# First group of a state-space decoder layer: two pairs of chunks from tokens without the row scale

## Chip, cores and metric

The kernel runs on one core of a Trainium2 chip. The metric is device time in microseconds, the median of three runs. Engines: PE (TensorE matmul, its weight loads shown as PEld), DVE (VectorE), ACT (ScalarE), POOL (GpSimd) and SP, whose queue issues all DMAs that matter here.

## What is computed

A decoder layer on 16 sequences of 256 tokens with 512 features, all float32, in three parts: a state-space block, a long convolution against a context, and a feed-forward layer with low-rank experts. The change lies in the start of the first part:

```python
xn = x * rsqrt(mean(x * x, axis=-1) + EPS) * w_norm       # row scale per token, wn per feature
proj = einsum('bld,td->blt', xn, W_in)
z, xi, dt, Bm, Cm = split(proj)                            # 1024, 1024, 16, 256, 256 columns
xi = silu(causal_conv4(xi))                                # per column, 4 taps along the tokens
dt = softplus(dt + dt_bias); dA = exp(-dt * exp(A_log))
u = (dt * mean of xi per head) * Bm
h = dA * h + u ; y = sum(h * Cm)                           # scan along the tokens
out = (y @ W_h2i.T * silu(z)) @ W_out.T + x                # then x + out, layer norm
```

The row scale is one number per token. It commutes with the product over features, so it can multiply the projected columns too.

## The kernel before

**Groups.** The first part runs over eight groups of 512 tokens (two sequences). In a group the projection is done with the tokens along the free axis: `xnT` holds the turned x, 128 features x 4 x 512 tokens. Columns are handled in pairs of 128-column chunks, in an order written out by hand; for the first group it is x0, x1, z0, x2, z1, x3, b0, c1, z2, z3 (L660 to L663). "x1" is the second pair of `xi` columns, with chunks 2 and 3, and so on.

**A pair.** Each pair is a 2 x 2 block product with seven products in place of eight: two chunks, two sequences, two halves of the features. `A11`, `S1`, `S2`, `S3`, `A12`, `S4`, `A22` are the weights and their sums, the S made by POOL in `weight_sums` (L259); "11", "12", "21", "22" are the quarters of xnT and T1 to T4 differences of them (L250 to L257). A product is four matmul instructions of 128 x 256 in the trace. `first_products` (L375) does A11, S1, S2, S3 into two PSUM banks `al`, `be`; `first_sums` (L385) reads them, one ACT copy and three DVE sums (L388, L389, L390); `last_products` (L393) adds A12, S4, A22 onto the same banks; `last_sums` (L399) reads them (ACT L400, DVE L401, L402).

**Order.** The scheduler is off: each engine executes in the order of the code. In iteration i of the loop at L686 PE gets the first products of pair i and then the last products of pair i-1; DVE gets the first sums of pair i, then the last sums of pair i-1 (`finish_sums`, L671). For an x pair `mixed` (L614) follows for both its chunks: the four-tap convolution, the first tap by DVE (L621, even chunk) or ACT (L619, odd chunk), three more by DVE (L623). `al` and `be` come from two pools: two banks for every third pair, four for the others.

**Weight sums of POOL.** Those of x0, x1, z0 and x2 are made in front, the others in iterations 1, 2 and 4, each behind a wait for the last L623 of a pair (L748).

**The front of the first group.** SP issues four DMAs of x rows (`xt`, L227, for the mean squares), `wn` (L269), the low and high half of the turned x with the first two weights between (L272 to L275), then w_z 0 and the rest. PE runs idle matmuls (L521). `rms` (L404) squares the rows on ACT and DVE and takes the power -1/2 on POOL (L419); `along_tokens` (L422) turns the scale into a PSUM tile `rt` that holds it along the free axis; `normed` (L444) multiplies xnT by wn and rt (L446). `decays` (L452) makes dt and dA, its matmuls `d` (L460) on PE in iteration 1, its further steps in iterations 2, 3 and 4.

Of the kernel before, what the change touches and what calls it, by code (L numbers as in the profile page):

```python
# [8 lines left out]
F32 = mybir.dt.float32  # L9
# [5 lines left out]
P = 128  # L15
# [10 lines left out]
GT = 512  # L26
# [27 lines left out]
)  # L54
ER = NE * R
NG = NE + ER
WARM = 8


def layer_norm_stats(nc, pool, nhalf, src, tag):  # L60
# [13 lines left out]
def decoder_kernel(  # L74
# [135 lines left out]
    with ExitStack() as s1:  # L210
# [12 lines left out]
        def load_x(g):  # L223
            xs = []
            for t in range(TT):
                xt = xp.tile([P, D], F32, tag="xt", name="xt")
                nc.sync.dma_start(xt, xg[g * TT + t])  # L227
                xs.append(xt)
            return xs
# [17 lines left out]

        A11, A12, A22, S3, S1, S2, S4 = range(7)

        def first_token_sum(eng):  # L250
            eng.tensor_tensor(Xs["T1"], Xs["12"], Xs["11"], ALU.subtract)  # L251

        def other_token_sums(eng):
            eng.tensor_tensor(Xs["T2"], Xs["22"], Xs["T1"], ALU.subtract)  # L254
            eng.tensor_tensor(Xs["T3"], Xs["22"], Xs["12"], ALU.subtract)

            eng.tensor_tensor(Xs["T4"], Xs["21"], Xs["T2"], ALU.subtract)  # L257

        def weight_sums(eng, w, p):  # L259

            ins = eng.tensor_tensor(w[:, p, S1], w[:, p, S3], w[:, p, A22], ALU.add)
            eng.tensor_tensor(w[:, p, S2], w[:, p, S1], w[:, p, A11], ALU.subtract)
            eng.tensor_tensor(w[:, p, S3], w[:, p, A11], w[:, p, S3], ALU.subtract)
            eng.tensor_tensor(w[:, p, S4], w[:, p, A12], w[:, p, S2], ALU.subtract)
            return ins

        xs_next = load_x(0)
        wn = wp.tile([P, KD], F32, name="wn")
        nc.sync.dma_start(wn, w_norm)  # L269
        w_xi = big.tile([P, NI // 2, 7, 2, P], F32, tag="big", name="w_xi")  # L270
        w_z = big.tile([P, NI // 2, 7, 2, P], F32, tag="big", name="w_z")
        nc.sync.dma_start(xnT[:, 0:2], xTg[:, 0:2, 0:GT])  # L272
        nc.sync.dma_start(w_xi[:, 0, 0:4], Wxi[:, 0])
        nc.sync.dma_start(xnT[:, 2:4], xTg[:, 2:4, 0:GT])
        nc.sync.dma_start(w_xi[:, 1, 0:4], Wxi[:, 1])  # L275
        nc.sync.dma_start(w_z[:, 0, 0:4], Wz[:, 0])
        for p in range(2, NI // 2):
            nc.sync.dma_start(w_xi[:, p, 0:4], Wxi[:, p])
# [74 lines left out]
        def bank():  # L353
            return ps_mm.tile([P, 512], F32, tag="mm", name="mm")

        def product(ps, w, p, a, b, start=False, stop=False, upon=False):
            for kc in range(2):
                nc.tensor.matmul(  # L358
                    ps,
                    w[:, p, a, kc, :],  # L360
                    Xs[b][:, kc, :],
                    start=start and kc == 0,
                    stop=stop and kc == 1,
                    skip_group_check=upon,
                )

        def begin_products(w, p, third):

            al, be = [
                ps_s.tile([P, 512], F32, tag="s", name="s") if third else bank() for _ in range(2)  # L370
            ]
            product(al[:, 0:S], w, p, A11, "11", start=True)
            return al, be

        def first_products(w, p, third, begun=None, between=None):  # L375

            al, be = begun or begin_products(w, p, third)
            product(be[:, 0:S], w, p, S1, "T1", start=True)
            if between is not None:
                between()  # L380
            product(al[:, S:], w, p, S2, "T2", stop=True)
            product(be[:, S:], w, p, S3, "T3", stop=True)
            return al, be
# [20 lines left out]
        def rms(xs, both=False):  # L404

            n = len(xs)
            ss = p2.tile([P, TT], F32, tag="ss", name="ss")[:, 0:n]
            for t in range(n):
                sq = p2.tile([P, D], F32, tag="acc", name="sq", bufs=6)
                if both and t % 2:  # L410
                    nc.vector.scalar_tensor_tensor(
                        sq, xs[t], 1.0, xs[t], ALU.mult, ALU.mult, accum_out=ss[:, t : t + 1]
                    )
                else:
                    nc.scalar.activation(sq, xs[t], AF.Square, accum_out=ss[:, t : t + 1])
            ms = p2.tile([P, TT], F32, tag="ms", name="ms")[:, 0:n]
            nc.vector.tensor_scalar(ms, ss, 1.0 / D, RMS_EPS, ALU.mult, ALU.add)  # L417
            rstd = p2.tile([P, TT], F32, tag="rstd", name="rstd")[:, 0:n]
            nc.gpsimd.tensor_tensor(rstd, ms, nhalf[:, 0:n], ALU.pow)  # L419
            return rstd  # L420

        def along_tokens(ps, rstd):  # L422

            for t in range(2):
                nc.tensor.matmul(
                    ps[:, t * P : (t + 1) * P],
                    rstd[:, t : t + 1].to_broadcast([P, P]),
                    ident,
                    start=True,
                    stop=True,  # L430
                )
# [12 lines left out]
        def normed(rt, kcs=range(KD)):  # L444
            for kc in kcs:
                nc.vector.scalar_tensor_tensor(  # L446
                    xnT[:, kc, :], xnT[:, kc, :], wn[:, kc : kc + 1], rt, ALU.mult, ALU.mult
                )
# [68 lines left out]
        def idle(n):  # L517

            ps = bank()
            for _ in range(n):  # L520
                nc.tensor.matmul(ps[:, 0:P], ident, ident, start=True, stop=True)  # L521


        rt = ps_t.tile([P, GT], F32, tag="tr", name="rt")
        idle(WARM)
        for b in range(GB):
            along_tokens(
                rt[:, b * S : (b + 1) * S], rms(xs_next[b * TT // GB : (b + 1) * TT // GB], True)
            )
            idle(WARM // 2)  # L530
        normed(rt, (0, 1))
        first_token_sum(nc.vector)
        normed(rt, (2, 3))
        other_token_sums(nc.vector)
        for w, p in ((w_xi, 0), (w_xi, 1), (w_z, 0), (w_xi, 2)):
            weight_sums(nc.gpsimd, w, p)

        later = {
            1: ((w_z, 1),), 2: ((w_xi, 3), (w_bc, 0), (w_bc, 1)), 4: ((w_z, 2), (w_z, 3)),
# [48 lines left out]
        for g in range(groups):  # L588
# [25 lines left out]
            def mixed(c):  # L614

                xi = xis[c % 4]
                acc = p2.tile([P, GB, S], F32, tag="acc", name="acc", bufs=6)
                if c % 2:
                    nc.scalar.activation(acc, xi[:, :, 3:], AF.Identity, scale=wc[:, c, 3:4])  # L619
                else:  # L620
                    nc.vector.tensor_scalar(acc, xi[:, :, 3:], wc[:, c, 3:4], None, ALU.mult)  # L621
                for k in range(2, -1, -1):
                    ins = nc.vector.scalar_tensor_tensor(  # L623
                        acc, xi[:, :, k : k + S], wc[:, c, k : k + 1], acc, ALU.mult, ALU.add
                    )
                mixes.append(ins)
                accs.append(acc)
                silus.append(acc)
# [33 lines left out]
                order[1:3] = order[2:0:-1]  # L662
            order += [("b", 0), ("c", 1), ("z", 2), ("z", 3)]  # L663
            before = None
            begun = []

            def finish_products():
                kind, p, al, be, u, to = before
                last_products(al, be, kinds[kind], p)
# [16 lines left out]
            for i, (kind, p) in enumerate(order):  # L686
# [4 lines left out]
                    sums.append((w, cols, chunk_sum(w, cols)))  # L691
                if i == 6:
                    ms = [head_means(0)]
                if g == 0 and i == 0:
                    al, be = first_products(
                        kinds[kind], p, True, None,
                        lambda: begun.append(begin_products(w_xi, order[1][1], False)),
                    )
                else:
                    al, be = first_products(  # L700
                        kinds[kind], p, i % 3 == 0, begun.pop(0) if begun else None
                    )
                if i == 8:
                    ms.append(head_means(1))
                if i == 9:
# [11 lines left out]
                            )  # L717
                    if sums:
                        centred(*sums.pop(0))
                if before is not None:  # L720
                    finish_products()
                to = places(kind, p)
                u = first_sums(al, be, to)
                if i == 8:
                    states(1, stepped(ms[1], spreads[2]), spreads[3])
                if i == 6:
                    ms = [stepped(ms[0], spreads[0])]
                    spreads.append(spread(1, 1))
                if g == 0:
                    if i == 1:  # L730
                        parts = decays()
                    if i == 2:
                        nc.scalar.activation(A, A, AF.Exp)
                        nc.vector.tensor_scalar(A, A, -1.0, None, ALU.mult)
                    if i in (1, 2, 4):
                        next(parts)
                if i == 9:
                    yT = q3.tile([P, S], F32, tag="vn", name="yT", bufs=1)
                    nc.scalar.copy(yT, yps)
                if before is not None:  # L740
                    finish_sums((lambda: next(parts)) if g == 0 and i == 2 else None)
                if g == 0 and i == 3:
                    next(parts)
                if g == 0 and i in later:
# [1024 lines left out]
```

## Time and profile before

| | |
|---|---|
| median of three runs | 1398.14 us (1397.74 to 1398.74) |
| profiled execution | 1399.62 us, its span 1397.8 us |
| PE busy | 1379.8 us |
| DVE busy | 1186.5 us |
| POOL busy | 620.2 us |
| ACT busy | 450.2 us |
| granted TensorE clock | 0.998 mean |

Three runs lie within 1 us. The profiled execution is one execution with the profiler on, from which all durations come; its span runs from the first to the last instruction. A busy PE is not PE at its peak, as matmuls overlap and their ends are modelled.

### The profile page before, as it was taken

The numbers are of one execution on the slowest core, as the hardware profiler recorded it, in microseconds if no ns is written. First come the engines' busy times: TensorE is split into PE (matmuls) and PEld (weight loads), VectorE is DVE, ScalarE is ACT, GpSimd is POOL, SyncE is SP. The second block draws the span as 40 slices with busy tenths as digits, with TensorE's granted clock in tenths as the row PEclk, the third lists the DMA queues.
The fourth block names the chain that finished last, engine by engine and source line by source line (L and its number), as shares of the span: only waits on it lengthen the run. The fifth ranks groups of instructions, "written<-read, shape, count | busy, mean of one in ns | idle before, by whom it ended". The sixth has DMA issues, their size and how long they took to land.

```text
span 1397.8 us, 19582 instructions
## 1 busy us (share of the span) xinstructions
PE 1379.8 (99%) x6967; PEld 935.3 (67%) x6967; DVE 1186.5 (85%) x2270; ACT 450.2 (32%) x979; POOL 620.2 (44%) x849
## 2 busy tenths in 40 slices
PE   8999999999999999999999999999999999999997
PEld 7888788788888887888886345445454454545444
DVE  6888879878788787788866889999999999999986
ACT  2524324243243342432421323333323333333232
POOL 5451021020100201001003768877888788887884
PEclk9999999999999999999999999999999999999999
DMA  8113212212113131121306554454543555345500
GB/s 307 34 38 91 63 54 37 69 40 55 39 41 68 49 68 39 41 53 42 80 20 87 69 69 64 60 74 61 76 64 60 74 76 76 61 61 72 65 27 38
DMA packets 362386, 89.48 MB, mean 64 GB/s; under 512 B 330032, under 2 KB 334512, under 8 KB 362288
## 3 DMA queue, kind: packets, MB, share of 16 engines
q1 hardware_dynamic: 362288, 88.23, 34.1%
q8 instruction: 55, 0.90, 0.3%
q14 instruction: 43, 0.35, 0.1%
HBM read 70.62 MB, written 17.58 MB: 63 GB/s over the span
## 4 chain that ended last, share of the span: by engine, by line
PE 94%; DVE 3%; issue 1%; DMA 1%; POOL 0%; ACT 0%; SPq 0%; POOLq 0%; DVEq 0%
PE mm L358 21%; PE y L1088 15%; PE s L358 14%; PE y L1103 12%; PE s L826 6%; PE mm L826 6%; PE y L1070 4%; PE be L1335 4%; PE al L1335 3%; PE gl L1280 2%; PE xm L634 1%; PE mm L783 1%; PE mm L920 1%; PE al L1307 1%; PE s L920 1%
## 5 line engine op out<-in xcount | busy, mean ns | idle before, releaser
L1136 DVE TENSOR_TENSOR pr<-y,cT 128x1024 f32<-128x1024 f32 x126 | 148.4, 1219 | 38.4 <-PE y L1103 37.7
L1103 PE MATMUL y<-kv 64*64 64x512 f32 x1536 | 179.6, 598 | 0.0
L187 DVE TENSOR_TENSOR kv<-tr,cT 128x1024 f32<-128x1024 f32 x128 | 150.0, 1212 | 0.8 <-ACT tr L179 0.8
L623 DVE SCALAR_TENSOR_TENSOR acc<-xi,wc,acc 128x512 f32<-128x512 f32 x192 | 142.8, 757 | 7.4 <-ACT acc L619 1.8
L1146 DVE TENSOR_REDUCE red<-pr 128x128 f32<-128x1024 f32 x126 | 147.1, 1208 | 0.0
L1088 PE MATMUL y<-kv 128*128 128x512 f32 x272 | 128.3, 594 | 3.5 <-DVE pr L1136 3.4
L1103 PEld LDWEIGHTS y<-kv 64*64 64x64 f32 x1536 | 52.2, 132 | 118.6 <-issue 96.7
L69 POOL TENSOR_TENSOR rs_a<-ve_a,nhalf 128x1 f32<-128x1 f32 x32 | 17.5, 546 | 255.3 <-DVE ve_a L67 255.0
L1088 PE MATMUL y<-kv,Td 128*128 128x512 f32 x248 | 116.5, 592 | 0.0
L419 POOL TENSOR_TENSOR rstd<-ms,nhalf 128x4 f32<-128x4 f32 (+1 forms) x9 | 8.6, 954 | 229.7 <-DVE ms L417 229.7
L358 PE MATMUL mm<-XT,w_z 128*128 128x256 f32 x384 | 90.7, 379 | 0.0
L1088 PEld LDWEIGHTS y<-kv,Td 128*128 128x128 f32 x248 | 47.1, 190 | 59.3 <-issue 59.3
L1077 ACT COPY y<-y 64x512 f32<-64x512 f32 x120 | 67.0, 558 | 59.5 <-PE y L1070 57.6
L1088 PEld LDWEIGHTS y<-kv 128*128 128x128 f32 x272 | 51.1, 189 | 44.9 <-ACT y L1077 17.3
L1054 POOL TENSOR_TENSOR xs<-kv 128x512 f32<-128x512 f32 x63 | 80.2, 1273 | 0.1
L358 PEld LDWEIGHTS mm<-XT,w_z 128*128 128x128 f32 x384 | 73.0, 190 | 9.9
L358 PE MATMUL mm<-xnT,w_z 128*128 128x256 f32 x288 | 70.8, 382 | 0.0
L1490 POOL TENSOR_TENSOR ol<-o,red 128x512 f32<-128x512 f32 x31 | 39.3, 1267 | 61.4 <-DVE red L1146 61.4
L251 POOL TENSOR_TENSOR XT<-xnT 128x512 f32<-128x512 f32 x7 | 9.3, 1326 | 129.0 <-PE mm L826 129.0
L1070 PE MATMUL y<-xs,kv 128*128 128x512 f32 x120 | 62.2, 600 | 0.4
L358 PE MATMUL s<-XT,w_xi 128*128 128x256 f32 x256 | 61.0, 380 | 0.8 <-DVE XT L254 0.5
L358 PEld LDWEIGHTS mm<-xnT,w_z 128*128 128x128 f32 x288 | 54.0, 190 | 10.1 <-issue 3.0
(337 smaller groups left out, 3065.6 us busy)
## 6 DMA issues: line engine op xcount, KB each, us to landing
cT<-in_ctxT SPq DMA_DIRECT2D x32, 384.0 KB
kv<-in_toep SPq DMA_DIRECT2D x32, 384.0 KB
xt<-in_x SPq DMA_DIRECT2D x32, 256.0 KB
spread<-both SPq DMA_DIRECT2D x32, 256.0 KB
first<-xt SPq DMA_DIRECT2D x124, 64.0 KB
vT<-first SPq DMA_DIRECT2D x31, 256.0 KB
out<-res SPq DMA_DIRECT2D x31, 256.0 KB
xnT<-in_xT SPq DMA_DIRECT2D x7, 1024.0 KB
```

The lines of the kernel that those rows point to most:

```text
L187: last = nc.vector.tensor_tensor(kv[:, q, k * BQ : (k + NL // 2) * BQ], vT[:, q, blks].rearrange("p k (b i) -> p (k b) i", i=NH).unsqueeze ...
L358: nc.tensor.matmul(ps, w[:, p, a, kc, :], Xs[b][:, kc, :], start=start and kc == 0, stop=stop and kc == 1, skip_group_check=upon,)
L623: ins = nc.vector.scalar_tensor_tensor(acc, xi[:, :, k : k + S], wc[:, c, k : k + 1], acc, ALU.mult, ALU.add)
L826: nc.tensor.matmul(ps, own[a][c][:, n * P : (n + 1) * P], w_o[b][c], start=start and c == 0, stop=stop and c == HC - 1, skip_group_check=upon,
L1054: return nc.gpsimd.tensor_tensor(xs[:, q], moving(kv, q, 0), moving(kv, q, 1), ALU.add)
L1070: nc.tensor.matmul(seed, T[:, SHARED_AT, :], xs[:, q], start=True, stop=True)
L1077: nc.scalar.copy(bank_of(y, 2)[b : b + HP], seed[a : a + HP])
L1088: nc.tensor.matmul(bank_of(y, lb), w, moving(kv, q, mb), start=not late and lb not in begun, stop=False, skip_group_check=True,)
L1103: return nc.tensor.matmul(bank_of(y, lb)[cols], T[rows, DIAGONAL_AT, (b - a) * HP : (b - a + 1) * HP], moving(kv, q, lb)[rows], start=star ...
L1136: nc.vector.tensor_tensor(pr.rearrange("p (k b j) i -> p k b j i", k=2, j=NH), y[i].rearrange("p k (b j i) -> p k b j i", j=NH, i=NH), cT[ ...
L1146: nc.vector.tensor_reduce(red[:, q, 2 * i : 2 * i + 2, :].rearrange("p k t -> p (k t)"), pr, AX.X, ALU.add)
L1335: nc.tensor.matmul(ps, a[:, kc, :], w[:, kc, :], start=(start and kc == 0), stop=(kc == 1), skip_group_check=True,)
```

## The change

Only the first group differs. The turned x is loaded first, into two tiles of its own (`x_lo`, `x_hi`), followed by wn and the first two weights between and behind the halves; the x rows come after these. ACT and DVE multiply the halves by wn, in place. T1 to T4 are made from them, and the pairs x0 and x1 take these tokens, without the row scale. Meanwhile the mean squares are taken on ACT and DVE, after x0's first sums; power and turning follow x0's last products on POOL and PE. POOL makes the weight sums of z0 and x2 behind the power. DVE then multiplies the four rows of tokens by rt into xnT and makes T1 to T4 again; T4 comes between x0's last sums and its `mixed`. The results of x0 and x1 are multiplied by rt in `mixed`, once for each of four chunks, by DVE. In iteration 2, x1's last products stand ahead of z0's first ones, and the `d` matmuls and first two steps of `decays` both fall there. x0's and x1's first products are no longer interleaved; 11 idle matmuls stand in front, and none between.

```diff
-WARM = 8
+WARM = 11
...
+        def given_tokens():
+
+            halves = [gp.tile([P, 2, GT], F32, tag="zs", name="xr") for _ in range(2)]
+            sums = [gp.tile([P, 2, GT], F32, tag="zs", name="xr_sum") for _ in range(2)]
+            X = {
+                f"{k + 1}{b + 1}": t[:, :, b * S : (b + 1) * S]
+                for k, t in enumerate(halves)
+                for b in range(GB)
+            }
+            for i in range(4):
+                X[f"T{i + 1}"] = sums[i // 2][:, i % 2, :].rearrange("p (k s) -> p k s", k=2)
+            return halves, X
...
-        xs_next = load_x(0)
         wn = wp.tile([P, KD], F32, name="wn")
-        nc.sync.dma_start(wn, w_norm)
+        (x_lo, x_hi), Xr = given_tokens()
...
-        nc.sync.dma_start(xnT[:, 0:2], xTg[:, 0:2, 0:GT])
+        nc.sync.dma_start(x_lo, xTg[:, 0:2, 0:GT])
+        nc.sync.dma_start(wn, w_norm)
         nc.sync.dma_start(w_xi[:, 0, 0:4], Wxi[:, 0])
-        nc.sync.dma_start(xnT[:, 2:4], xTg[:, 2:4, 0:GT])
+        nc.sync.dma_start(x_hi, xTg[:, 2:4, 0:GT])
         nc.sync.dma_start(w_xi[:, 1, 0:4], Wxi[:, 1])
+        xs_next = load_x(0)
         nc.sync.dma_start(w_z[:, 0, 0:4], Wz[:, 0])
...
+        unscaled = {0, 1}
+
         def product(ps, w, p, a, b, start=False, stop=False, upon=False):
+            X = Xr if w is w_xi and p in unscaled else Xs
...
-        rt = ps_t.tile([P, GT], F32, tag="tr", name="rt")
         idle(WARM)
-        for b in range(GB):
-            along_tokens(
-                rt[:, b * S : (b + 1) * S], rms(xs_next[b * TT // GB : (b + 1) * TT // GB], True)
-            )
-            idle(WARM // 2)
-        normed(rt, (0, 1))
-        first_token_sum(nc.vector)
-        normed(rt, (2, 3))
-        other_token_sums(nc.vector)
-        for w, p in ((w_xi, 0), (w_xi, 1), (w_z, 0), (w_xi, 2)):
-            weight_sums(nc.gpsimd, w, p)
+        for k, t in enumerate((x_lo, x_hi)):
+            nc.scalar.activation(t[:, 0, :], t[:, 0, :], AF.Copy, scale=wn[:, 2 * k : 2 * k + 1])
+            nc.vector.tensor_scalar(
+                t[:, 1, :], t[:, 1, :], wn[:, 2 * k + 1 : 2 * k + 2], None, ALU.mult
+            )
+            if k == 0:
+                first_token_sum(nc.vector, Xr)
+        middle_token_sums(nc.vector, Xr)
+        last_token_sum(nc.vector, Xr)
+        for p in range(2):
+            weight_sums(nc.gpsimd, w_xi, p)
+
+        def scaled_tokens(rt, k):
+
+            for e, t in enumerate(((x_lo, x_hi)[k][:, i, :] for i in range(2))):
+                nc.vector.tensor_tensor(xnT[:, 2 * k + e, :], t, rt, ALU.mult)
...
+                if c // 2 in unscaled:
+                    nc.vector.tensor_tensor(
+                        xi[:, :, 3:], xi[:, :, 3:], rt.rearrange("p (b s) -> p b s", b=GB), ALU.mult
+                    )
                 if c % 2:
                     nc.scalar.activation(acc, xi[:, :, 3:], AF.Identity, scale=wc[:, c, 3:4])
...
+                if g == 0 and i == 2:
+                    finish_products()
+                al, be = first_products(kinds[kind], p, i % 3 == 0)
...
-                if before is not None:
+                if before is not None and (g or i != 2):
                     finish_products()
+                if g == 0 and i == 1:
+                    rt = ps_t.tile([P, GT], F32, tag="tr", name="rt")
+                    along_tokens(rt, inverse_root(mean_squares))
+                    for w, k in ((w_z, 0), (w_xi, 2)):
+                        weight_sums(nc.gpsimd, w, k)
                 to = places(kind, p)
                 u = first_sums(al, be, to)
+                if g == 0 and i == 0:
+                    mean_squares = rms(xs, True)
+                if g == 0 and i == 1:
+                    scaled_tokens(rt, 0)
+                    first_token_sum(nc.vector)
+                    scaled_tokens(rt, 1)
+                    middle_token_sums(nc.vector)
...
                 if g == 0:
-                    if i == 1:
+                    if i == 2:
                         parts = decays()
+                        next(parts)
...
-                    if i in (1, 2, 4):
+                    if i in (2, 4):
                         next(parts)
...
-                    finish_sums((lambda: next(parts)) if g == 0 and i == 2 else None)
+                    between = {1: lambda: last_token_sum(nc.vector), 2: lambda: next(parts)}
+                    finish_sums(between.get(i) if g == 0 else None)
+                if g == 0 and i == 2:
+                    unscaled.clear()
```

`inverse_root` is the last step of `rms`, the power on POOL, now a function of its own; `middle_token_sums` makes T2 and T3, `last_token_sum` T4.

More of the change, by code (lines that the diff above doesn't have):

```diff
@@ L248, in decoder_kernel, with first_token_sum, middle_token_sums, last_token_sum @@
         A11, A12, A22, S3, S1, S2, S4 = range(7)
-        def first_token_sum(eng):
-            eng.tensor_tensor(Xs["T1"], Xs["12"], Xs["11"], ALU.subtract)
+        def given_tokens():
[9 more added lines that the diff above has]
+            return halves, X
+        def first_token_sum(eng, X=None):
+            X = X or Xs
+            eng.tensor_tensor(X["T1"], X["12"], X["11"], ALU.subtract)
+        def middle_token_sums(eng, X=None):
+            X = X or Xs
+            eng.tensor_tensor(X["T2"], X["22"], X["T1"], ALU.subtract)
+            eng.tensor_tensor(X["T3"], X["22"], X["12"], ALU.subtract)
+        def last_token_sum(eng, X=None):
+            X = X or Xs
+            eng.tensor_tensor(X["T4"], X["21"], X["T2"], ALU.subtract)
         def other_token_sums(eng):
-            eng.tensor_tensor(Xs["T2"], Xs["22"], Xs["T1"], ALU.subtract)
-            eng.tensor_tensor(Xs["T3"], Xs["22"], Xs["12"], ALU.subtract)
-            eng.tensor_tensor(Xs["T4"], Xs["21"], Xs["T2"], ALU.subtract)
+            middle_token_sums(eng)
+            last_token_sum(eng)
         def weight_sums(eng, w, p):
@@ L360, in product @@
                     w[:, p, a, kc, :],
-                    Xs[b][:, kc, :],
+                    X[b][:, kc, :],
                     start=start and kc == 0,
@@ L365, in product, with first_products @@
                 )
-        def begin_products(w, p, third):
+        def first_products(w, p, third):
             al, be = [
@@ L372, in begin_products @@
             product(al[:, 0:S], w, p, A11, "11", start=True)
-            return al, be
-        def first_products(w, p, third, begun=None, between=None):
-            al, be = begun or begin_products(w, p, third)
             product(be[:, 0:S], w, p, S1, "T1", start=True)
-            if between is not None:
-                between()
             product(al[:, S:], w, p, S2, "T2", stop=True)
@@ L417, in rms, with inverse_root @@
             nc.vector.tensor_scalar(ms, ss, 1.0 / D, RMS_EPS, ALU.mult, ALU.add)
+            if both:
+                return ms
+            return inverse_root(ms)
+        def inverse_root(ms):
+            n = ms.shape[1]
             rstd = p2.tile([P, TT], F32, tag="rstd", name="rstd")[:, 0:n]
@@ L422, in along_tokens @@
         def along_tokens(ps, rstd):
-            for t in range(2):
+            for t in range(TT):
                 nc.tensor.matmul(
@@ L664, in decoder_kernel @@
             before = None
-            begun = []
             def finish_products():
@@ L693, in decoder_kernel @@
                     ms = [head_means(0)]
[L694 to L697, printed above, removed]
-                    )
[L699 to L702, printed above, removed]
+                if g == 0 and i == 2:
+                    finish_products()
+                al, be = first_products(kinds[kind], p, i % 3 == 0)
                 if i == 8:
```

## Prediction

> **What bounds the kernel now.** I read the page first: busy time by engine.
>
> ```profile
> PE 1379.8 (99%) x6967; PEld 935.3 (67%) x6967; DVE 1186.5 (85%) x2270; ACT 450.2 (32%) x979; POOL 620.2 (44%) x849
> ```
>
> TensorE is the bound over the whole span, so a microsecond that it loses anywhere ends up in the time. The next view is the chain of waits over the first 60 us, for where TensorE starts to be the bound (start, length, what).
>
> ```profile
> 2.10 5.76 DMA xt<-in_x
> ...
> 10.51 1.42 DVE xnT L446 x2
> ...
> 14.06 1.17 DVE XT L254
> 15.37 1.10 PE s L358 x4
> ...
> 17.60 2.59 PE mm L358 x12
> 20.19 2.59 PE s L358 x12
> 22.78 1.01 PE d_lg L460 x32
> ```
>
> Until 15.4 us the chain goes over the x rows, their scale and the T sums; then it stays on PE. Twelve instructions take 2.59 us, 0.216 each. One product of the code is four of them (0.86 us), so a pair's four first products take 3.45, its three last ones 2.59. By 22.78 PE has done 44 instructions, 9.5 us, as if it had started at 13.3 and never waited.
>
> The third view asks what stands just behind PE: VectorE's timeline of the first group, with PE's weight loads for the same stretch.
>
> ```profile
> 22.82 0.42 DVE L401 TENSOR_TENSOR xi<-u,s 128x256 f32<-128x256 f32 x1 [1.65 <-PE s L358]
> ...
> 36.43 2.33 DVE L623 SCALAR_TENSOR_TENSOR acc<-xi,wc,acc 128x512 f32<-128x512 f32 x3 [1.75 <-ACT acc L619]
> 38.67 0.41 DVE L388 TENSOR_TENSOR u<-u,s 128x256 f32<-128x256 f32 x1
> 39.19 0.42 DVE L389 TENSOR_TENSOR xi<-u,s 128x256 f32<-128x256 f32 x1
> 39.65 0.42 DVE L390 TENSOR_TENSOR xi<-xi,s 128x256 f32<-128x256 f32 x1
> ```
> ```profile
> 39.15 1.70 PEld L358 LDWEIGHTS s<-xnT,w_xi 128*128 128x128 f32 x8
> ...
> 46.22 0.73 PEld L358 LDWEIGHTS mm<-xnT,w_z 128*128 128x128 f32 x4 [0.19 <-DVE zs L390]
> ...
> 53.53 0.73 PEld L358 LDWEIGHTS mm<-xnT,w_xi 128*128 128x128 f32 x4 [0.21 <-DVE xi L390]
> ```
>
> This decides the case. A pair's last products add onto the same PSUM banks that its first sums (L388 to L390) still read: the first last product must wait for L388, the second for L390. From 22.8 us on VectorE has almost no gap. For pair x2 its L390 ends at 40.07, and PE's second last product starts about 40.4, its weight load 0.2 earlier. For z1 and x3 PE's weight load already waits for L390. So in the first group VectorE is a second bound with no reserve by pair x2; only around z0 is there slack (L390 ends at 29.99, PE's second last product comes at about 34).
>
> **The change part by part.**
>
> *DMA order.* In the SP queue's own waits and timeline each issue from the eleventh on waits for the transfer eight places before it. So the starts of those issues give landings: third xt 7.2, x low half 9.2, first w_xi 10.6, x high half 11.9, second w_xi 13.2; 512 KB each 1.3 us. The same bytes go out in another order, so I take the landing of the same position: x low half 4.4 to 5.2 (where two xt landed: 4.4), w_xi 0 at 7.9 (fourth xt), x high half 9.2, w_xi 1 at 10.6, the four xt 11.2 to 13.2; w_z 0 and all behind it as now. The tiny wn now stands second; it only has to be there by about 7. SP issues nothing more.
>
> *Start.* Scaling the low half is one ACT and one DVE instruction side by side (ACT 0.72, the L619 row; DVE 0.5 to 0.6, L621), T1 is 0.77: all before 7.9. PE: x0's A11 product at 7.9, S1 at 8.8 (POOL's sum 0.73). The high half is scaled by 10.0. T2, T3, T4 follow beside POOL's weight sums, at the 1.16 to 1.21 each that L254 to L257 took beside POOL now: T2 at 11.2, T3 at 12.3. So PE does S2 at 11.2, S3 at 12.3 and then runs: x1 first to 16.6, x0 last to 19.2.
>
> *Row scale.* Squares and mean come behind x0's first sums: VectorE is there at 14.9 (T4 to 13.4, three sums 1.4), two squares 1.6, ms at 16.6; POOL's pow 0.72, done at 17.4. PE reaches the turning of rstd at 19.2, so nothing waits for it. Its eight instructions (four in 0.78 now, idle matmuls 0.13 each when quick) take 1.2: rt at 20.4, after VectorE has idled since 18.
>
> *Tokens with scale.* From 20.4 on VectorE: two multiplications 1.4 (0.68 each, the row with PSUM input L645), T1 1.1 (beside POOL), two more 1.4, T2 0.8, T3 0.75: 25.85. Meanwhile PE does x1 last (20.4 to 23.0), z0's A11 and S1 (to 24.7), waits 0.4 for T2 (25.1), ends z0 first at 26.9, d at 27.9, x2 first at 31.4. Without a wait PE would now be ahead of before by 2.0 us: before had z0 first, d and x1 last done at 29.8, after has them at 27.9.
>
> *What it leaves for VectorE.* Before, x0's last sums start at 22.82; after, at 25.85: 3.0 later. From there to x2's first sums (before 38.67, 15.85 us later) the change adds T4 0.75, four multiplications by rt 3.0 (L645's 0.68 and its gap, 0.75 each), and a new wait: ACT's L619 for each odd chunk can start only behind the multiplication, and VectorE, which had run the even chunk's four instructions meanwhile, waits 0.75. In x1 that replaces the 1.75 wait of the trace. Sum: 0.75 + 3.0 + 0.75 + 0.75 - 1.75 = 3.5. So VectorE reaches x2's first sums 3.0 + 3.5 = 6.5 us late: L388 at 45.2, L390 ends at 46.6.
>
> *Where PE stands then.* z0's first sums come at 34.6 to 35.9; PE wants z0's last products at 31.4: a wait of 3.2, and a little more for L390. z0 last ends at 37.5, z1 first at 41.2 (x1's banks come free at 37.7; w_z 1 sums, which wait for x0's mixing, are ready by then). x2's last products then wait for L388 until 45.6 and for L390 until 46.6, against 40.4 before: PE is 6.2 late, and by z1 and x3, where PE waits for L390 already, the full 6.5. POOL's w_xi 3 sums wait for the same mixing and have about 3 us in hand either way. What follows is the same work in the same order, and PE is the bound to the end: nothing gives it back. I take 6.4.
>
> [...] Three of the T sums gate the start. Beside POOL they took 1.21 against 0.77 alone, POOL's sums 1.17 against 0.73. [...] The multiplications with PSUM input are not slowed: L446 took 0.74 with POOL busy.
>
> Second, the granted clock reads 1.00 from the first slice, yet the 16 idle matmuls took 3.79 us (0.24 each) and only the last eight 1.06. [...]
>
> **The rivals.**
> 1. *PE alone decides* (faster, or no change): the first sums come in time, and only the 2.0 us of the earlier start are left: about 1396.1. For it: PE carries 94% of the chain. Against: the two L390 waits. It needs VectorE to be 6 us earlier than worked out; to gain over 2.8 it also has to lose no time to T2 and T3.
> 2. *Half of it*: transfers land 1 us sooner, T1 runs undisturbed, or multiplications and ACT overlap better. The loss is 2 to 4: 1400 to 1402.
> [...]
> 4. *The early start does not come*: the halves of x or wn land late. VectorE's extra work stays, and each microsecond that T2 comes late puts rt, and all behind it, a microsecond later: 1405.5 to 1408 for one to three and a half. Against: the first two xt landed at 4.4 from the same place in the queue.
>
> **The numbers.** The profiled execution took 1399.62 with a span of 1397.80; the median of the three runs is 1398.14, 1.5 below it. A span of 1397.8 + 6.4 = 1404.2 is a median of 1404.5. Chances: the VectorE chain at 4.5 to 8 late 0.64; half of it 0.14; rivals 3 and 4 beyond that 0.10; PE alone 0.12, of it a third beyond 2.8 us (0.2%, about what a measurement of this kernel can tell from no change). From half of it a fraction lies inside 2.8. Range 1400.0 to 1408.0: it leaves out PE alone and the far end of rivals 3 and 4. Faster 0.05, same 0.13, slower 0.82.
>
> **What would show it.** Right: x0's first product at about 8 instead of 11.3; PE idle for some 3 us before z0's last products and some 4 before x2's, released by VectorE's first sums; VectorE without gaps from 20 to 46 but for two ACT waits; x2's first sums near 45. Wrong: no PE wait for the first sums in the first group, or x2's first sums before 42; then the time is below 1401.

## The result, and the profile after

The changed kernel takes 1404.89 us (median of 6, 1403.04 to 1405.76) against 1398.32 before (median of 6): 6.6 us slower, a ratio of 1.0048 with a 95% interval of 1.0037 to 1.0058. The prediction was 1404.5, slower. Its profiled execution took 1405.69, with a span of 1402.8. In the span the loss is 5.0, in the profiled executions' times 6.1, and in the medians 6.6. To measure one mechanism, the text below compares instants inside the traces. The profiled execution of before took 1399.62, which is 1.3 above its median; where its trace lost that time is told at the end of the part on the prediction.

The busy times of the page hardly move:

```profile
PE 1380.9 (98%) x6957; PEld 936.0 (67%) x6957; DVE 1190.6 (85%) x2279; ACT 451.7 (32%) x981; POOL 621.3 (44%) x848
```

VectorE gained 4 us of work in 1190. That total does not place the loss; the chain of waits of the first 60 us does (start, length, what):

```profile
2.19 6.81 DMA xr<-in_xT
...
10.85 1.10 PE s L383 x4
...
19.13 0.91 PE rt L450 x8
...
20.06 1.29 DVE xnT L565 x2
...
40.66 0.73 ACT acc L652
...
43.74 0.34 DVE u L406
44.08 0.04 issue
44.12 4.54 PE s L383 x12
48.67 6.04 PE mm L383 x28
```

Before, the chain stayed on PE from 15.4 on. Now, behind the transfers of x and the turning of rt, it leaves PE at 20.06 and runs over VectorE and ACT for 24 us, back to PE at 44.12. And the row before the last holds a second thing: twelve instructions took 4.54 us, where twelve took 2.59 before. The timeline shows both pauses of PE, in its matmul rows (PE) and its weight loads (PEld). In the changed kernel L383 is a product, and L406 to L408 are the first sums, which were L388 to L390 before.

```profile
33.69 0.73 PEld L383 LDWEIGHTS mm<-xnT,w_z 128*128 128x128 f32 x4 [3.07 <-DVE u L406]
33.69 3.14 PE L383 MATMUL mm<-xnT,w_z 128*128 128x256 f32 x8 [2.67 <-DVE u L406]
...
44.12 2.61 PEld L383 LDWEIGHTS s<-xnT,w_xi 128*128 128x128 f32 x8 [2.84 <-DVE u L406]
44.12 3.33 PE L383 MATMUL s<-xnT,w_xi 128*128 128x256 f32 x8 [2.44 <-DVE u L406]
```

Both are last products (z0's and x2's) that wait for the first sums of their own pair, as forecast. Before, x2's came without a pause:

```profile
39.36 1.89 PE L358 MATMUL s<-xnT,w_xi 128*128 128x256 f32 x8
```

VectorE's timeline, with the last sums of x0, the first multiplication by rt, the wait for ACT, and the first sums of z0 and x2:

```profile
24.77 0.41 DVE L419 TENSOR_TENSOR xi<-u,s 128x256 f32<-128x256 f32 x1
...
26.03 0.68 DVE L648 TENSOR_TENSOR xi<-xi,rt 128x512 f32<-128x512 f32 x1
...
30.98 2.33 DVE L656 SCALAR_TENSOR_TENSOR acc<-xi,wc,acc 128x512 f32<-128x512 f32 x3 [0.79 <-ACT acc L652]
33.22 0.41 DVE L406 TENSOR_TENSOR u<-u,mm 128x256 f32<-128x256 f32 x1
...
43.66 0.41 DVE L406 TENSOR_TENSOR u<-u,s 128x256 f32<-128x256 f32 x1
```

x2's first sums start at 43.66, against 38.67 before: 5.0 us late. But the second group's `xnT` load, far behind them, is 6.4 late. Its issue before, and after:

```profile
79.09 0.40 SPq L246 DMA_DIRECT2D xnT<-in_xT  x1
```
```profile
85.51 0.40 SPq L246 DMA_DIRECT2D xnT<-in_xT  x1
```

The other 1.4 is the clock. Stretches of the changed kernel, and the second of them before (the columns are the length, the busy time of PE, PEld, DVE, ACT and POOL with their instructions, then the granted clock, the DMA share and GB/s):

```profile
34.40:37.80 3.40, 3.40 (x9) 2.62 (x9) 3.29 (x10) 1.76 (x3) 1.94 (x3) 0.50 0.01 2
37.80:41.00 3.20, 3.20 (x16) 2.80 (x16) 2.75 (x4) 3.17 (x6) 0.00 (x0) 1.00 0.00 0
41.00:44.60 3.60, 1.16 (x6) 0.71 (x5) 3.01 (x5) 2.07 (x5) 0.73 (x1) 1.00 0.00 0
44.60:48.00 3.40, 3.40 (x10) 2.72 (x9) 3.27 (x8) 2.51 (x4) 3.29 (x5) 0.50 0.00 0
```
```profile
44.60:48.00 3.40, 3.40 (x17) 2.70 (x15) 3.23 (x8) 1.79 (x5) 3.13 (x5) 1.00 0.09 21
```

The third last column is the granted clock. It reads 0.50 in two stretches, each just behind a pause. In them PE is "busy" throughout, but with 9 and 10 instructions, where the kernel before has 17 in the stretch of the same length. The kernel before has 1.00 all through its first group. The sum closes: x2's last products start 4.76 late (44.12 against 39.36), and 3.4 us at half clock behind them cost 1.7, which makes 6.5 for the 6.4 found. The first stretch cost nothing that can be seen, as PE had to wait for VectorE again behind it.

### The profile page after: what moved, and what is told of

Its sections match the earlier page's. It is cut to its first block, busy times and chain, and to the rows that moved or that the text cites. A ratio compares the mean times of both kernels' runs of the same rounds, so it can differ in the third digit from the quotient of the medians.

```text
span 1402.8 us, 19573 instructions
## 1 busy us (share of the span) xinstructions
PE 1380.9 (98%) x6957; PEld 936.0 (67%) x6957; DVE 1190.6 (85%) x2279; ACT 451.7 (32%) x981; POOL 621.3 (44%) x848
## 4 chain that ended last, share of the span: by engine, by line
PE 93%; DVE 4%; issue 1%; ACT 1%; DMA 1%; POOL 0%; SPq 0%; POOLq 0%; DVEq 0%; ACTq 0%
PE mm L383 20%; PE y L1130 15%; PE s L383 14%; PE y L1145 12%; PE s L868 6%; PE mm L868 6%; PE y L1112 4%; PE be L1377 4%; PE al L1377 3%; PE gl L1322 2%; PE xm L667 1%; PE mm L825 1%; PE mm L962 1%; PE al L1349 1%; PE s L962 1%
## 5 line engine op out<-in xcount | busy, mean ns | idle before, releaser
L444 POOL TENSOR_TENSOR rstd<-ms,nhalf 128x4 f32<-128x4 f32 x8 | 8.2, 1027 | 224.6 <-DVE ms L435 224.6
L383 PE MATMUL mm<-XT,w_z 128*128 128x256 f32 x384 | 91.5, 381 | 0.1
L383 PEld LDWEIGHTS mm<-XT,w_z 128*128 128x128 f32 x384 | 73.5, 192 | 10.5 <-issue 0.4
L383 PE MATMUL mm<-xnT,w_z 128*128 128x256 f32 x288 | 71.9, 386 | 2.7 <-DVE u L406 2.7
L383 PEld LDWEIGHTS mm<-xnT,w_z 128*128 128x128 f32 x288 | 54.6, 192 | 13.2 <-DVE u L406 3.1
L383 PE MATMUL s<-XT,w_xi 128*128 128x256 f32 x240 | 57.1, 381 | 0.0
```

The source lines that it names most:

```text
L383: nc.tensor.matmul(ps, w[:, p, a, kc, :], X[b][:, kc, :], start=start and kc == 0, stop=stop and kc == 1, skip_group_check=upon,)
```

## The experiments

The theory: VectorE is a second bound in the first group, so its delay at x2's first sums is PE's; and a pause of PE can bring a stretch at half clock, which comes on top. The main rival was that PE has reserve and something else (the clock alone, POOL, the DMA order) makes the loss. Each kernel is the changed one with an edit, but for the first, which starts from the kernel before. Two instants are read from each trace: the start of x2's first sums against 38.67 (VectorE's delay), and the issue of the second group's xnT load against 79.09, called the shift, as everything behind it moves with it. The ratios are against the kernel before, run at the same time.

**More VectorE work in the kernel before.**

```diff
+                if g == 0 and c < 2:
+                    for _ in range(2):
+                        nc.vector.tensor_tensor(
+                            spare, xi[:, :, 3:], rt.rearrange("p (b s) -> p b s", b=GB), ALU.mult
+                        )
```

> The kernel before with four more VectorE multiplications of 128x512 by the row scale in PSUM, two behind each of x0's chunks in the first group, their results unused: 2.8 to 3.0 of VectorE work. Theory (VectorE is a second bound in the first group): x2's first sums end 2.9 later, PE waits for them, 1398.3 + 2.7 = 1401.0, up to 1402.7 if the pause brings a half-clock stretch. Rival (PE has reserve): 1398.3, no change.

1401.71 us against 1397.89, a ratio of 1.0023 (1.0014 to 1.0033). Nothing of the change is in this kernel, only four more instructions, whose results nobody reads. Its VectorE and PE rows, and its stretch behind the pause:

```profile
40.25 0.41 DVE L388 TENSOR_TENSOR u<-u,s 128x256 f32<-128x256 f32 x1
```
```profile
40.72 3.63 PE L358 MATMUL s<-xnT,w_xi 128*128 128x256 f32 x8 [2.11 <-DVE u L388]
```
```profile
40.70:44.10 3.40, 3.38 (x8) 2.75 (x9) 3.23 (x8) 2.37 (x5) 3.27 (x5) 0.50 0.02 5
```

PE had no reserve: the rival falls. The delay at x2 is 1.6, not the 2.9 expected; this execution's front was 0.9 us quicker (x0's first sums stand at 16.49 instead of 17.41). The xnT load is 3.0 late, so half clock made up the rest. The ten runs fall apart into five from 1400.07 to 1401.34, with a mean clock of 0.998 or 0.999, and five from 1402.09 to 1402.66, with 0.997 or 0.998. The traced one, 1402.09, is of the second kind; the first kind may have had no stretch at half clock, but none of it was traced.

**PE kept busy through its pauses.**

```diff
...
+            for _ in range(warm):
+                nc.tensor.matmul(al[:, 0:P], ident, ident, start=True, stop=True)
             product(al[:, 0:S], w, p, A11, "11", start=True)
```

`warm` is 12 ahead of x2's first products and 18 ahead of z1's, in the first group.

> Adds 12 and 18 idle matmuls on PE ahead of x2's and z1's first products, where PE would otherwise pause later; VectorE's work is untouched. Theory: the pauses before z0's and x2's last products are filled, the granted clock stays full, and of the two half-clock stretches of 3.4 us only the second cost time: 1.7 back, 1403.2, the shift against before 4.7 instead of 6.4; VectorE's first sums of x2 stay near 43.7. Rival (the clock does not matter, VectorE alone sets it): same as the changed kernel, 1404.9. Rival (idle matmuls get in the way): slower by up to 3.

1403.30, ratio 1.0035 (1.0022 to 1.0048). The same stretches as above:

```profile
34.40:37.80 3.40, 3.40 (x21) 2.82 (x20) 3.33 (x9) 1.57 (x3) 2.12 (x3) 1.00 0.01 3
...
44.60:48.00 3.40, 3.40 (x17) 2.79 (x17) 3.30 (x8) 2.37 (x4) 3.24 (x6) 1.00 0.00 0
```

The clock stays full, VectorE's first sums of x2 are nearly where they were (43.85), and the shift is 5.0: what is left is VectorE's delay of 5.2, to 0.2 us. By the trace, work that computes nothing took 1.4 us off the changed kernel's shift; the intervals of the two ratios overlap, so the times alone would not show it.

**Only the second pause filled.** The same edit with the 18 matmuls ahead of z1 alone.

> Of the idle matmuls only the 18 ahead of z1's first products are kept, so the pause before z0's last products stays empty. Theory: the first half-clock stretch is back but costs nothing, as PE waits for VectorE again behind it; the second is gone: same as with both fillings, 1403.3, shift 5.0 in the first part. Rival (the first stretch costs its own 1.7): 1405.

1404.57 (1402.65 to 1406.21), ratio 1.0047 (1.0034 to 1.0060). It could not answer its question. In the profiled execution PE paused before z0's last products as in the changed kernel (its weight load waited 3.1 us), yet the clock stayed full:

```profile
31.00:34.40 3.40, 1.06 (x5) 0.75 (x5) 3.19 (x8) 0.00 (x0) 1.28 (x2) 1.00 0.56 204
34.40:37.80 3.40, 3.40 (x24) 3.09 (x24) 3.29 (x8) 2.10 (x4) 1.59 (x3) 1.00 0.02 6
```

So a pause of this length (2.7 us in PE's matmul row, in both kernels) was followed by half clock in the traced execution of the changed kernel and not in this one. The shift is 4.6, again VectorE's delay (x2's first sums at 43.31). The traced run took 1402.85 at a mean clock of 0.999; three of the five took 1404.57 to 1406.21 at 0.996 to 0.998, so a stretch at half clock may have cost those some 2 us, but they were not traced. What the first stretch costs by itself stays open.

**Without the multiplications of the results.** The `if c // 2 in unscaled` block in `mixed` taken out, so that x0 and x1 lack the row scale.

> Left out: the four multiplications of the results of x0 and x1 by the row scale, so these columns lack it. Theory (VectorE reaches the first sums of x2 late, and PE's pause before them brings a stretch at half clock): VectorE saves the two multiplications of x0 (1.4) and ACT's wait (0.8); those of x1 are mostly hidden behind ACT's table loads, whose wait of some 1.8 comes back. x2's first sums at 41.5 instead of 43.7, no wait left before z0's last products; a pause of some 4 before x2's, so a half-clock stretch of 1.7 may stay. Time 1401 to 1403. Rival (the multiplications are the whole loss): all but the start's gain comes back, 1396 to 1398. Rival (half clock alone): no change if the stretch stays.

1403.03, ratio 1.0032 (1.0020 to 1.0045): at the upper end of what the theory gave, and the multiplications are not the whole loss. x2's first sums start at 41.35, still 2.7 late. PE's weight load before x2's last products waits longer, 4.3 us, as PE lost less before z0; half clock now begins within this pause and lasts from 40.1 to 47.0. The shift is 4.95.

**Row scale turned earlier.**

```diff
             product(al[:, 0:S], w, p, A12, "21", upon=True)
+            if between is not None:
+                between()
...
```

For x0's last products `between` issues rt's matmuls.

> The turning of the row scale goes onto PE after the first of x0's three last products instead of behind all three; nothing is left out. Theory: rt is there at 18.5 instead of 20.06, VectorE's idle stretch before it shrinks by some 1.6, and everything behind on VectorE comes 1.6 sooner: x2's first sums at 42.1, time 1403.3; with a shorter pause the half clock before z0 may not come. Rival (VectorE's start doesn't count, as PE's own work or ACT sets the later waits): 1404.9.

1404.43, ratio 1.0047 (1.0034 to 1.0059): a miss. VectorE did come 0.9 sooner at x2 (42.72; rt was used from 18.66 on, 1.4 sooner, but T3, 0.68 in the changed kernel, now ran beside POOL's sums and took 1.21). But the clock took most of it back:

```profile
41.00:44.60 3.60, 1.41 (x3) 1.17 (x4) 3.39 (x8) 1.26 (x3) 1.64 (x3) 0.54 0.00 0
44.60:48.00 3.40, 3.40 (x9) 2.70 (x8) 3.23 (x8) 2.38 (x4) 3.32 (x5) 0.50 0.00 0
```

Half clock begins at 41.3, before PE resumes at 43.2, and lasts to 48.1: a shift of 6.2 with a VectorE delay of 4.05.

**Both together.** The early turning, with 7 and 18 idle matmuls ahead of x2's and z1's first products.

> Row scale turned after the first of x0's last products, together with 7 and 18 idle matmuls ahead of x2's and z1's first products; nothing is left out. Theory (VectorE's delay and half clock add up): no half clock, x2's first sums at 42.7, a shift of 4.0 to 4.2 in the first part, 1402.3. Rival (the early turning has no effect of its own): shift 5.0, 1403.3.

1402.09, ratio 1.0026 (1.0016 to 1.0036). The traced execution has a mean granted clock of 0.999, as the one with both pauses filled, no pause in PE's matmul row behind the front, x2's first sums at 42.65 and a shift of 3.97. Against the version with the pauses filled alone, the early turning is worth 1.1 us by the traces; the intervals of the two times overlap.

**Multiplications on POOL.**

```diff
-                    nc.vector.tensor_tensor(
-                        xi[:, :, 3:], xi[:, :, 3:], rt.rearrange("p (b s) -> p b s", b=GB), ALU.mult
-                    )
+                    nc.gpsimd.tensor_tensor(xi[:, :, 3:], xi[:, :, 3:], rts, ALU.mult)
...
+                    nc.scalar.copy(rts, rt.rearrange("p (b s) -> p b s", b=GB))
```

> The four multiplications of the results by the row scale go from VectorE to POOL; ACT copies rt from PSUM to SBUF for them. Nothing is left out. [...] Rival (POOL's 1.3 for a multiplication puts a new wait in front of VectorE): x2's first sums at 44 or later, 1405 or more.

1406.08, ratio 1.0064 (1.0050 to 1.0077), above the changed kernel's 1.0048, though the intervals overlap. By the theory x2's first sums come at 41.5 to 42.5, and the time is 1403 to 1404: a miss. VectorE's T4, the first tap of x0's first chunk, and its wait in x1:

```profile
25.83 1.53 DVE L274 TENSOR_TENSOR XT<-xnT,XT 128x512 f32<-128x512 f32 x1
27.29 1.31 DVE L652 TENSOR_SCALAR acc<-xi,wc 128x512 f32<-128x512 f32 x1
...
37.45 1.29 DVE L652 TENSOR_SCALAR acc<-xi,wc 128x512 f32<-128x512 f32 x1 [1.02 <-POOL xi L648]
```

T4 took 0.68 and the tap 0.49 in the changed kernel; here both ran beside POOL's first two multiplications (2.58 us, from 25.73 on). VectorE's work on the tokens also began 0.33 later, at 20.39, behind ACT's copy of rt. These delays and the new wait for POOL ate nearly all that was saved (x2's first sums at 43.43), and half clock from 42.9 to 49.7 did the rest: a shift of 7.4.

**All of it.** POOL's multiplications, early turning, x0's `mixed` behind z0's first sums and x1's last sums, 14 idle matmuls.

> Everything that the runs point to at once: multiplications on POOL, row scale turned after the first of x0's last products, x0's mixing on VectorE put behind z0's first sums and x1's last sums, 14 idle matmuls ahead of z1's first products. Nothing is left out. Theory: no pause before z0, x2's first sums at 39.5 to 40.5 against 38.67 in the kernel before, full clock: a shift of 1 to 2, 1399 to 1400. It does not beat the kernel before, because VectorE's total work ahead of x2's first sums is what counts. Rival (order alone frees PE, the 2 us of the early start come through): 1396.

1403.10, ratio 1.0039 (1.0027 to 1.0052). The pause before z0 is gone (first sums at 27.21), but x2's come at 42.42, not 39.5 to 40.5: beside POOL's next two multiplications the six further taps of x0 took 5.98 instead of the 4.66 of the changed kernel. A pause of 2.1 and a stretch at half clock followed. The order alone did not free PE; of the versions tried, none beat the kernel before without leaving work out.

**VectorE relieved.** The multiplications taken out, and with them two of the three further taps of each of x0's and x1's chunks in the first group:

```diff
-                for k in range(2, -1, -1):
+                for k in range(2, 1 if g == 0 and c < 4 else -1, -1):
```

> Left out: the four multiplications by the row scale and, for the four chunks of x0 and x1 in the first group, two of the three further taps of the convolution (eight VectorE instructions of 0.76). Everything else of the change stays. Theory (the early start gives PE 2.4, and only VectorE takes it away): x2's first sums come before PE wants them (36 against 37), no pause, no half clock, the shift in the first part is -2.0 to -2.4, the time 1395.5 to 1396. Rival (POOL's weight sums, the DMA order or the later d matmuls hold PE back too): no better than the kernel before, 1397.8.

1396.17 against 1398.23, ratio 0.9984 (0.9976 to 0.9992). The early start, the DMA order, POOL's sums and the moved `d` matmuls are all still there. x2's first sums start at 36.49, PE's last products at

```profile
36.95 2.11 PE L383 MATMUL s<-xnT,w_xi 128*128 128x256 f32 x8
```

against 39.36 before; the shift is -2.2. Their weight load still waited 0.4 us for the first sums, but PE's matmul row shows no pause, and the granted clock reads 1.00 from 31 to 48. This is the gain that the change aims at, and VectorE's extra work stood in its way.

All kernels in one table (us; half clock read from the granted clock in steps of 0.4 us):

| kernel | x2's first sums, late by | half clock about | shift of the xnT load |
|---|---|---|---|
| changed | 5.0 | 34.4 to 37.8, 44.6 to 48.0 | 6.4 |
| without multiplications | 2.7 | 40.1 to 47.0 | 5.0 |
| pauses filled | 5.2 | none | 5.0 |
| turned early | 4.05 | 41.3 to 48.1 | 6.2 |
| turned early, filled | 4.0 | none | 4.0 |
| on POOL | 4.8 | 42.9 to 49.7 | 7.4 |
| all of it | 3.75 | 44.3 to 47.7 | 5.3 |
| second pause filled | 4.6 | none | 4.6 |
| before, four more | 1.6 | 40.7 to 44.1 | 3.0 |
| VectorE relieved | -2.2 | none | -2.2 |

Without half clock the shift equals VectorE's delay within 0.2 in all four; with it, 1.4 to 2.6 come on top. How much depends on where the stretch lies. In the six kernels with half clock, the late start of x2's last products (against 39.36) plus half of the slow time behind that start gives the shift within 0.1 us: slow time within a pause costs nothing, slow time behind it costs half its length. Without the multiplications, for instance, they start at 41.82, 2.46 late, and the slow time from there to 46.96 costs 2.57: together 5.03, where 4.96 was found.

## Why the prediction was right, and where it was not

*Start.* Right: first product at 7.8 (said 7.9), T2 at 10.7 (11.2), x0's last products done at 19.1 (19.2), rt at 20.06 (20.4). VectorE beside POOL came about as the trace of the kernel before had it: T3 took 1.21 beside POOL's sums, where that trace has 1.16 to 1.21, and T2 0.92. One reading was off: the T sum of 0.77 that it calls alone (L251) ran beside POOL as well, whose own sum took 1.18 there; T1 alone took 0.69 in the changed kernel.

*PE ahead without a wait.* Right in kind: x2's first products start at 27.3, against 29.9 before with the same work behind PE. That is 2.6 ahead, where 2.0 was said; the wait of 0.4 for T2 did not come.

*VectorE's delay.* Right in kind, 6.5 said and 5.0 found. The terms: x0's last sums 25.85 said, 24.77 found, since rt came 0.35 sooner, T2 and T3 took 0.6 each instead of 0.8 and 0.75, T1 0.95 instead of 1.1, and the multiplications in pairs 1.28, not 1.4. From there to x2's first sums 19.3 said, 18.9 found. The 0.75 for ACT's wait was 0.79, twice.

*The waits.* Right in place: before z0's and x2's last products, both behind the first sums. Their length was 2.7 and 2.4 on PE, where 3.2 and 4.4 were worked out: VectorE was earlier, and half clock stretched PE's own work between them.

*The clock.* This step failed. The prediction's sum has no half clock: none behind the pauses of the front, where the clock in fact held (1.0 and 1.1 us in PE's matmul row, the granted clock 1.00 from 3 to 34.4), and none behind the two pauses of 3.2 and 4.4 that it had just worked out itself. What came is a stretch of 3.4 us at half clock behind each of them, and 1.4 us of loss. The two pauses measured 2.7 and 2.4 us. Their length alone does not settle it, as the other pause of 2.7, in the run with only the second pause filled, brought no half clock. So it was luck that the sum of 6.4 for the shift was met: two errors of about 1.5 cancel, VectorE's delay too long and the clock left out. No run shows what the third rival, which has part of the 0.10 in the chances, stands for; in its place the runs showed T3 at 1.21 and T2 at 0.92 beside POOL, and half clock for 3.4 us behind two pauses.

*Nothing gives it back.* Nearly right: the shift is 6.4 in every group of the first part. In the change to the second part, between 746 and 772 us, it falls to 5.5, and it falls by 0.8 to 0.9 in every other variant too, the one with the opposite sign included (from -2.2 to -3.1). There PE pauses 2.03 us before and 1.13 after for VectorE, and ACT, ahead of it, waits 5.5 us before and 4.5 after for the `vT` transfer. Towards the end of the span another 0.5 goes, which leaves the 5.0 of the spans. Since all variants share the first fall, also the kernel before with four more instructions, it belongs to the one profiled execution of before rather than to the change; the two falls together, 1.4, fit the 1.3 by which that execution was above its median. Why that transfer came later there stays open.

## What to carry to other kernels

When one engine is busy all the time, look at who releases its buffers. Here weight loads that waited 0.19 and 0.21 us for a release, where the matmul row showed no gap, pointed to a second bound. Work added to that engine then cost nearly its full length, although the first engine is the one that is 99% busy: the four multiplications added to the kernel before, 2.8 us, made VectorE 2.5 us longer from x0's last sums to x2's first ones. An early start is worth having only if the engine behind it gets no extra work before its own next deadline; count that engine's queue from the moved step to the deadline, instruction by instruction. And price each wait of PE that you forecast twice: its length, and the slow clock that PE may have behind it (1.4 to 2.6 us in these traces).

## What was not expected of the hardware

In the first group of these traces, half clock follows pauses of PE in its matmul row in this way. The three of 3.9 to 4.0 us (without the multiplications, turned early, on POOL) came with 6.8 to 6.9 us at half clock each, which began within the pause. Of the six between 2.1 and 2.7 us, four were followed by one stretch of 3.4 us, and two (2.7 us in one trace, 2.2 us before z0 in another) by none. The pauses of 1.0 and 1.1 us in the front of the changed kernel and the one of 1.7 us before z0 in the version turned early were followed by a granted clock of 1.00.

In the changed kernel the two stretches begin at 34.4 and 44.6, 0.7 and 0.5 us after PE has resumed (33.69 and 44.12). What decides whether a pause of 2.1 to 2.7 us brings one was not shown.

The mean clock differs between runs of one kernel, too: of the changed kernel's six, the quickest (1403.04) has 0.997 and the others 0.995 or 0.996. The kernel before is not free of it: of 21 runs of it beside the last experiments, most took 1397.4 to 1398.4, and five 1400.0 to 1400.2 at 0.997. Those were not traced; a pause of 2.0 us at 763.5 in its trace left the clock full.
